# The third block of experts with up to 288 columns, computed in four quarters of the result's columns

## The chip, the cores and the metric

The kernel runs on one core of one Trainium2 chip. The metric is device time in microseconds (us) of one execution, as the median of several runs. The core's engines are named as in the profile: PE (TensorE, matmuls; PEld is its weight load), DVE (VectorE), ACT (ScalarE), POOL (GpSimd, which issues the indirect DMAs) and SP (SyncE, which issues the plain DMAs).

## What is computed

A macaron block over 8192 tokens (8 sequences of 1024) with 512 features, all in f32:

```python
x = x + 0.5 * ffn(layernorm(x))       # 32 experts, top-1, capacity 320
x = x + attention(layernorm(x))       # 16 heads of 32, rope, softmax
x = x + 0.5 * ffn(layernorm(x))       # the same experts again
```

The feed-forward part is where the change lies. Each token goes to the expert with the highest router probability, if it is among the first C = 320 tokens of that expert:

```python
C = ceil(1.25 * T / E)                                  # T = 8192, E = 32: 320
g = einsum("ech,ehf->ecf", buf, w_gate)
u = einsum("ech,ehf->ecf", buf, w_up)
y = einsum("ecf,efh->ech", silu(g) * u, w_down)
out_tok = where(accepted, y[slot] * gate, 0.0)
return xt + out_tok
```

All of H and F are 512. An expert's weights are three matrices of 512x512.

## The kernel before

The program has five parts in a row: a front that normalizes all tokens, computes the router's logits and writes a table of which token sits in which slot of which expert; a first expert stage; attention, which also routes the tokens for the second stage; a second expert stage; and nothing after it. The change touches only the expert stages.

**Widths.** The experts are sorted by their number of tokens, largest first (`sorted`). The number of columns of the expert of rank r is fixed when the program is built, in three lists (`Block.profiles`, lines 67 to 71); a value computed from the counts selects the first list that is wide enough (`arm`), and a switch (line 519) runs that one of three copies of the stage. With C = 320 and q = 32 the first list is ten experts of 320 columns, nine of 288, eight of 256 and five of 224; the second has only 320 and 256; the third only 320.

**Blocks.** An expert's tokens are taken in blocks of 128 partitions (`gather`, three indirect DMAs for over 256 columns, two else). A third block holds at most 64 tokens. So that its 128 partitions are used, the 64 tokens are there twice: `places` (line 554) reads the slot table as `rows`, copies the first 64 slots of each expert's third block over its last 64 (line 567), sorts it with a matmul against a permutation `matrix` (line 570), and writes three tables from the result: `come` (which token each partition gathers), `gates` (its gate), and `go` (which row of the output it writes). In the third block, partition half i writes row `2*token + i` of the output seen as rows of 256 (lines 574 to 579).

**One expert** (`feed`, line 712). PE's order is written out by hand, as is that of ACT, DVE and POOL (`manual_schedule`). For each of four slices f of the hidden columns: eight 128x128 weight tiles, four each for gate and up, as stationary operand, streamed against the transposed tokens `bT` (line 704, moving operand as wide as the expert), silu on ACT, and the product `a[:, f, :]` on DVE (line 728). Between f = 0 and f = 1 the next expert is normalized (`scales`, `normalize`), after f = 1 its `rests` are made. Then, block by block: six transposes of the next expert's tokens (line 692, before blocks 0 and 1), and the down product `yp`. In a full block `a` is the stationary operand, 128x128, and a slice of `wd` of 512 columns the moving one (line 745, four matmuls). In the third block (lines 751 to 757) `a`'s 64 columns are the stationary operand, once for each half of the result: half c of `wd`'s columns gives output partitions c*64 to c*64+63, 256 columns wide, so eight matmuls. DVE adds gate times `yp` to the residual (line 749; line 759 for the third block, with `rest`), and POOL scatters the 128 rows to the output (line 763).

**Rests** (line 669). The residual with its normalization is x scaled and shifted, per row. For full blocks it is made in place; for the third block, each half of the partitions takes its half of the columns into `rest` (two DVE instructions of 64x256).

**The start of a stage** (`experts`, lines 528 to 535). `places`, `gather` of expert 0, its weights, `begin` (statistics, normalization, twelve transposes at line 607, the copies to `bT` at line 611, and its rests), `gather` of expert 1, and then the loop over 32 experts with `feed`.

Of the kernel before, what the change touches and what calls it, by code (L numbers as in the profile page):

```python
# [13 lines left out]
F32 = mybir.dt.float32  # L14
# [3 lines left out]
ALU = mybir.AluOpType  # L18
# [4 lines left out]
P = 128  # L23
# [27 lines left out]
class Block:  # L51


    def __init__(self, nc, tc, T, D, E, F):
        self.nc, self.tc = nc, tc
        self.T, self.D, self.E, self.F = T, D, E, F
        self.NT, self.KD, self.KF = T // P, D // P, F // P
        self.C = int(math.ceil(CAPACITY_FACTOR * T / E))

        self.NB = -(-self.C // P)  # L60
        self.last = self.C - (self.NB - 1) * P
        assert E * self.NB <= P and self.last * 2 == P and D % 2 == 0
        self.NS = self.NB * E * P


        C, q = self.C, P // 4
        self.profiles = [
            [C] * 10 + [C - q] * 9 + [C - 2 * q] * 8 + [C - 3 * q] * (E - 27),
            [C] * 20 + [C - 2 * q] * (E - 20),
            [C] * E,  # L70
        ]
        assert all(widths[0] == widths[1] == C for widths in self.profiles)
        assert all(a <= b for one, two in zip(self.profiles, self.profiles[1:])
                   for a, b in zip(one, two))

        self.copy = nc.scalar.copy

# [424 lines left out]
    def experts(self, table, ranks, src, dst, weights, loaded=None, others=None):  # L502

        nc, tc, E = self.nc, self.tc, self.E
        views = dram_disjoint_views(dst, E * self.NB + (self.NT if others else 0))
        F = mybir.EngineType
        matrix, order, arm = ranks
        which = nc.values_load(
            arm[0:1, 0:1], min_val=0, max_val=len(self.profiles) - 1,
            skip_runtime_bounds_check_because="a sum of so many comparisons",
        )
        for i in tc.Switch(which, len(self.profiles)):
            widths = self.profiles[i]  # L520
            with (
                tc.tile_pool(name="ew", bufs=2) as wp,
                tc.tile_pool(name="ea", bufs=2) as ap,
                tc.tile_pool(name="eps", bufs=2, space=PSUM) as ps,
                tc.manual_schedule(engines={F.PE, F.Activation, F.DVE, F.Pool}),
            ):
                expert = Expert(self, (wp, ap, ps), src, views, others)
                expert.places(table, matrix)


                now = expert.gather(0, widths[0])
                now.weights = loaded or self.load(wp, order, 0, weights, hold="wu")
                expert.begin(now)
                following = expert.gather(1, widths[1])
                for r in range(E):
                    if following:
                        following.weights = self.load(
                            wp, order, r + 1, weights, hold=None if r else "wg"
                        )
                    after = None  # L540
                    if r + 2 < E:
                        after = lambda: expert.gather(r + 2, widths[r + 2])
                    now, following = following, expert.feed(now, following, after)


class Expert:
# [7 lines left out]
    def places(self, table, matrix):  # L554


        nc, s, ap, n = self.nc, self.s, self.ap, self.s.last
        E, R = s.E, s.NB * s.E
        self.come, self.go = (
            ap.tile([P, R], I32, tag=name, bufs=1, name=name) for name in ("come", "go")  # L560
        )
        ids, self.gates = (
            ap.tile([P, R], F32, tag=name, bufs=1, name=name) for name in ("ids", "gates")
        )
        rows = ap.tile([R, P, 2], F32, tag="slots", bufs=1, name="slots")
        nc.sync.dma_start(rows, table[0 : s.NS, :].rearrange("(r s) c -> r s c", s=P))
        nc.vector.tensor_copy(rows[R - E : R, n:P, :], rows[R - E : R, 0:n, :])
        for i, at in enumerate((ids, self.gates)):
            pt = self.ps.tile([P, R], F32, tag="tp", name="pt")
            nc.tensor.matmul(pt, rows[:, :, i], matrix, start=True, stop=True)  # L570
            if i == 0:
                nc.vector.tensor_scalar(self.come, pt, float(s.T - 1), None, ALU.min)
            nc.vector.tensor_copy(at, pt)
        nc.vector.tensor_copy(self.go[:, 0 : R - E], ids[:, 0 : R - E])
        for i in range(2):
            p = slice(i * n, (i + 1) * n)
            nc.vector.tensor_scalar(
                self.go[p, R - E : R], ids[p, R - E : R], 2.0, float(i), ALU.mult, ALU.add
            )

    def begin(self, to):

# [85 lines left out]

    def rests(self, to):

        s, n, half = self.s, self.s.last, self.s.D // 2
        for i in range(min(to.NB, s.NB - 1)):
            s.rest(to.x[:, i, :], to.x[:, i, :], to.by, i)
        if to.NB == s.NB:
            to.rest = self.ap.tile([P, half], F32, tag="rest", name="rest")
            for i in range(2):
                p = slice(i * n, (i + 1) * n)
                s.rest(
                    to.rest[p, :], to.x[p, s.NB - 1, i * half : (i + 1) * half], to.by,
                    s.NB - 1, p,  # L680
                )

# [29 lines left out]
    def feed(self, now, following, after):  # L712

        nc, s = self.nc, self.s
        n, half, KF = s.last, s.D // 2, s.KF
        a, wd = s.acts[now.r % 2], now.weights[2]
        others = self.fetch_others(now.r) if self.others else None
        if following:  # L720
            self.measure(following)
        later = after and after()
        for f in range(KF):
            sg, up = self.gated(now, f)
            if following and f == 0:
                self.scales(following)
                self.normalize(following)
            nc.vector.tensor_tensor(a[:, f, 0 : now.width], sg, up, ALU.mult)  # L728
            if following and f == 1:
                self.rests(following)  # L730
        if others:
            self.put_others(now.r, others)
        for i in range(now.NB):


            if following and i < 2:
                self.transpose(following, range(i * s.KD // 2, (i + 1) * s.KD // 2))
            yp = self.ps.tile([P, s.D], F32, tag="yp", name="yp")
            ys = self.ap.tile([P, s.D], F32, tag="ys", bufs=3, name="ys")
            gate = self.gates[:, i * s.E + now.r : i * s.E + now.r + 1]  # L740
            index = self.go[:, i * s.E + now.r : i * s.E + now.r + 1]
            to = self.views[now.r * s.NB + i]
            if i < s.NB - 1:
                for f in range(KF):
                    nc.tensor.matmul(  # L745
                        yp, a[:, f, i * P : (i + 1) * P], wd[:, f, :],
                        start=(f == 0), stop=(f == KF - 1),
                    )
                nc.vector.scalar_tensor_tensor(ys, yp, gate, now.x[:, i, :], ALU.mult, ALU.add)  # L749
            else:  # L750
                for f in range(KF):
                    for c in range(2):
                        nc.tensor.matmul(  # L753
                            yp[c * n : (c + 1) * n, 0:half], a[:, f, i * P : s.C],
                            wd[:, f, c * half : (c + 1) * half],
                            start=(f == 0), stop=(f == KF - 1),
                        )
                ys = ys[:, 0:half]
                nc.vector.scalar_tensor_tensor(
                    ys, yp[:, 0:half], gate, now.rest, ALU.mult, ALU.add  # L760
                )
                to = to.rearrange("t (c d) -> (t c) d", c=2)
            nc.gpsimd.indirect_dma_start(
                out=to, out_offset=bass.IndirectOffsetOnAxis(ap=index, axis=0),
                in_=ys, in_offset=None, bounds_check=to.shape[0] - 1, oob_is_err=False,
            )
        return later
# [730 lines left out]
```

## Time and profile before

| what | value |
|---|---|
| median of 3 runs | 4838.47 us (4837.74 to 4840.27) |
| the profiled execution | 4848.97 us |
| its span, first to last instruction | 4847.2 us |
| mean granted clock of PE | 0.974 |
| PE busy | 4596.5 us |
| DVE busy, ACT busy, POOL busy | 2836.3, 2923.5, 790.4 us |
| matmul records of line 753 (third block) | 608, busy 74.0 us together |
| matmul records of line 745 (full blocks) | 1024, busy 460.3 us together |
| DVE line 759 (third block's result) | 38, 483 ns each |
| DVE line 186, rest of 64x256 | 76, 412 ns each |

How to read the profile: times are counted from the span's start. The page divides the span into 40 slices and gives each engine's busy share of a slice in tenths. A line of the timeline has its start, its length, the engine, the line of the kernel, the operation, the tiles (out<-in), the shape and how many instructions were joined in it. An f32 matmul stands as two records of MATMUL and two of LDWEIGHTS. The shape `128*64 128x256` means 128 rows and 64 columns of stationary operand, and a moving operand of 256 columns. In brackets stands how long the engine was idle before, and what ended that. The chain is the work that ended last, followed back from the end: its shares say which engine and line set the time.

### The profile page before, as it was taken

How to read it: one execution, taken by the hardware profiler on the slowest of the kernel's cores; microseconds unless marked ns; L12 is line 12 of the kernel's file. 1: busy time of each engine (PE TensorE's matmuls, PEld its weight loads, DVE VectorE, ACT ScalarE, POOL GpSimd, SP SyncE). 2: the span in 40 equal slices, each digit the busy share in tenths (PEclk: the TensorE clock that was granted, in tenths of full speed). 3: DMA queues.
4: the chain of work that ended last, by engine and by line, in shares of the span. 5: the costliest groups of instructions: out<-in, count | busy, mean ns of one | idle time of the engine just before them, and what ended most of it. 6: DMA issues, size and time to landing. Idle time of an engine off the chain costs nothing.

```text
span 4847.2 us, 68820 instructions
## 1 busy us (share of the span) xinstructions
PE 4596.5 (95%) x24572; PEld 2128.0 (44%) x24572; DVE 2836.3 (59%) x5568; ACT 2923.5 (60%) x5856; POOL 790.4 (16%) x787
## 2 busy tenths in 40 slices
PE   6699999968999999999999999999999886999999
PEld 4466667722233333333333333333333234666677
DVE  8433333356666767767777767767767744333332
ACT  6221212128998888888888888888888841111111
POOL 4433333210000010110110110110110002222221
PEclk8799999979999999999999999999999997999999
DMA  4455566521111212212212212212212124455554
GB/s 142 148 187 184 190 197 220 178 85 29 34 30 60 75 38 65 70 42 65 70 42 65 70 42 65 69 42 66 60 43 57 49 70 154 158 174 177 171 193 137
DMA packets 290581, 486.02 MB, mean 100 GB/s; under 512 B 47895, under 2 KB 83169, under 8 KB 290224
## 3 DMA queue, kind: packets, MB, share of 16 engines
q1 hardware_dynamic: 255376, 404.36, 26.8%
q0 software_dynamic: 34560, 76.93, 5.2%
q8 instruction: 196, 3.21, 0.3%
q14 instruction: 161, 1.32, 0.1%
q10 hardware_dynamic: 288, 0.20, 0.0%
HBM read 380.11 MB, written 89.72 MB: 97 GB/s over the span
## 4 chain that ended last, share of the span: by engine, by line
PE 82%; DVE 7%; ACT 4%; issue 3%; DMA 2%; POOL 1%; SPq 1%; another core or an unknown queue 0%; DVEq 0%; POOLq 0%; ACTq 0%
PE sa L1220 13%; PE gp L704 10%; PE up L704 9%; PE pq L1125 9%; PE po L1302 9%; PE yp L745 9%; PE sb L1200 6%; PE px L1328 4%; PE pv L1170 4%; PE sb L1227 3%; ACT junk L1239 2%; DVE nm L1235 2%; PE tp L194 2%; DMA table<-row,slot 1%; PE yp L753 1%
## 5 line engine op out<-in xcount | busy, mean ns | idle before, releaser
L1235 DVE TENSOR_REDUCE nm<-sa 128x2 f32<-128x1024 f32 x1024 | 1248.7, 1220 | 648.3 <-PE sa L1220 386.9
L1239 ACT ACTIVATE junk<-sa,nm 128x512 f32<-128x512 f32 x2048 | 1407.3, 687 | 257.6 <-DVE nm L1235 177.0
L1220 PE MATMUL sa<-k,q 32*128 32x512 f32 x4096 | 1149.1, 645 | 17.9 <-ACT junk L1239 11.1
L1232 ACT ACTIVATE pr<-sb 128x1024 f32<-128x1024 f32 x1024 | 1040.5, 1018 | 101.3 <-PE sb L1227 97.4
L1227 PE MATMUL sb<-q,k 32*128 32x512 f32 x4096 | 1062.1, 602 | 0.0
L709 ACT ACTIVATE sg<-gp 128x320 f32<-128x320 f32 (+3 forms) x256 | 102.6, 401 | 1166.2 <-PE gp L704 1164.2
L1150 POOL TENSOR_TENSOR raw<-raw,a 128x512 f32<-128x512 f32 x128 | 164.2, 1283 | 2401.7 <-DMA rot<-raw 1645.0
L1302 PE MATMUL po<-pr,v 128*32 128x512 f32 x4096 | 548.0, 606 | 0.1
L704 PE MATMUL gp<-bT,wg 128*128 128x320 f32 (+3 forms) x2048 | 530.7, 402 | 0.0
L704 PE MATMUL up<-bT,wu 128*128 128x320 f32 (+3 forms) x2048 | 524.8, 399 | 0.0
L1125 PE MATMUL pq<-hT,wqk 128*128 128x512 f32 x1024 | 511.3, 624 | 4.9 <-DVE raw L1140 3.9
L745 PE MATMUL yp<-wd,a 128*128 128x512 f32 x1024 | 460.3, 592 | 0.0
L704 PEld LDWEIGHTS gp<-bT,wg 128*128 128x128 f32 x2048 | 386.7, 190 | 115.7 <-issue 26.7
L1200 PE MATMUL sb<-mrow,ones 3*128 3x512 bf16 x2048 | 392.9, 384 | 42.0 <-ACT pr L1232 40.7
L728 DVE TENSOR_TENSOR a<-sg,up 128x320 f32<-128x320 f32 (+3 forms) x256 | 114.0, 445 | 541.6 <-PE up L704 371.1
L704 PEld LDWEIGHTS up<-bT,wu 128*128 128x128 f32 x2048 | 388.9, 190 | 94.1
L1200 PEld LDWEIGHTS <-ones 3*128 3x128 bf16 x2048 | 99.6, 91 | 709.6 <-issue 670.1
L1239 ACT ACTIVATION_READ_ACCUMULATOR junk<-sa,nm 128x1 f32 x2048 | 398.2, 194 | 0.0
L1227 PEld LDWEIGHTS sb<-q,k 32*128 32x128 f32 x4096 | 359.7, 184 | 0.1
L1220 PEld LDWEIGHTS sa<-k,q 32*128 32x128 f32 x4096 | 304.9, 184 | 81.3 <-ACT pr L1232 30.3
L1125 PEld LDWEIGHTS pq<-hT,wqk 128*128 128x128 f32 x1024 | 176.2, 191 | 323.8 <-issue 227.0
L749 DVE SCALAR_TENSOR_TENSOR ys<-yp,gates,x 128x512 f32<-128x512 f32 x128 | 96.1, 751 | 336.8 <-PE yp L745 336.8
(178 smaller groups left out, 4241.8 us busy)
## 6 DMA issues: line engine op xcount, KB each, us to landing
wg<-in_w_gate SPq DMA_DIRECT2D x64, 1024.0 KB
wu<-in_w_up SPq DMA_DIRECT2D x64, 1024.0 KB
wd<-in_w_down SPq DMA_DIRECT2D x64, 1024.0 KB
rot<-raw SPq DMA_DIRECT2D x1024, 32.0 KB
all<-in_x SPq DMA_DIRECT2D x32, 512.0 KB
xt<-first_rows SPq DMA_DIRECT2D x64, 256.0 KB
xr<-first_rows SPq DMA_DIRECT2D x64, 256.0 KB
d<-inverse SPq DMA_DIRECT2D x256, 64.0 KB
```

The costliest lines, as they stand in the source:

```text
L704: nc.tensor.matmul(acc, w[:, k, f * P : (f + 1) * P], to.bT[:, k, 0:width], start=(k == 0), stop=(k == s.KD - 1),)
L745: nc.tensor.matmul(yp, a[:, f, i * P : (i + 1) * P], wd[:, f, :], start=(f == 0), stop=(f == KF - 1),)
L1125: nc.tensor.matmul(acc, w[:, which, k, :], self.hT[b, n][:, k, :], start=(k == 0), stop=(k == KD - 1),)
L1170: nc.tensor.matmul(acc, hT[:, k, at : at + P], self.w_vo[:, k, :], start=(k == 0), stop=(k == KD - 1),)
L1200: nc.tensor.matmul(sb[:, h, :], self.ones16[at : at + 3, :], row[at : at + 3, :], start=True, stop=False,)
L1220: nc.tensor.matmul(sa[:, h, :], qa[at, (g * 4 + j) * P : (g * 4 + j + 1) * P], ka[at, m * 512 : (m + 1) * 512], start=True, stop=True,)
L1227: nc.tensor.matmul(sb[:, h, :], k[at, t * P : (t + 1) * P], q[at, n * 512 : (n + 1) * 512], start=False, stop=True,)
L1232: nc.scalar.activation(pr, sb, AF.Exp)
L1235: nc.vector.tensor_reduce(nm[:, m, j, pair : pair + 2], sa, AX.X, ALU.max, negate=True)
L1239: nc.scalar.activation(self.junk, sa[:, h - pair, :], AF.Exp, bias=nm[:, m, j, h : h + 1], accum_out=se[:, m, j, h : h + 1],)
L1302: nc.tensor.matmul(self.po[at : at + HD, :], self.v[b][t][:, c * P + at : c * P + at + HD], prs[h // 2 * 2][:, h % 2, :], start=(t == 0), ...
L1328: nc.tensor.matmul(acc, self.oT[b, c, half][:, j * P : (j + 1) * P], self.w_vo[:, c, :], start=False, stop=(c == KD - 1),)
```

## The change

A third block with at most 32 tokens (an expert of at most 288 columns, `quarter`) has its tokens there four times, once for each quarter of the result's columns. `parts(width)` is 1, 4 or 2: 1 up to 256 columns, 4 up to 288, else 2. In the first list of widths the nine experts of 288 columns are concerned; in the other lists none.

- `places` is as before; a new step, `quarters`, follows after the gather of expert 1. It repeats the first 32 slots of the third blocks four times, sorts them with two small matmuls for the ranks concerned only, and writes these ranks' columns of `come`, `go` (`4*token + k` for partition quarter k) and `gates` again.
- `rests` makes four pieces of 32x128 instead of two of 64x256 for these experts.
- In `feed` the third block's product is, for these experts, sixteen matmuls with a stationary operand of 128x32 and a moving operand of 128 columns, each into 32 output partitions; the result is 128x128, and its rows are scattered into the output seen as rows of 128.

```diff
+        self.quarter = (self.NB - 1) * P + P // 4
...
                 following = expert.gather(1, widths[1])
+                expert.quarters(widths)
...
+    def parts(self, width):
+        s = self.s
+        return 1 if width <= (s.NB - 1) * P else 4 if width <= s.quarter else 2
+
+    def quarters(self, widths):
...
+        few = [r for r, width in enumerate(widths) if self.parts(width) == 4]
+        if not few:
+            return
...
+        rows = ap.tile([R, 4, n * 2], F32, tag="four", bufs=1, name="four")
+        nc.vector.tensor_copy(
+            rows[last, :, :],
+            self.rows[last, 0:n, :].rearrange("r s c -> r (s c)").unsqueeze(1)
+            .to_broadcast([E, 4, n * 2]),
+        )
+        rows = rows.rearrange("r k (s c) -> r (k s) c", c=2)
+        for i in range(2):
+            pt = self.ps.tile([P, len(few)], F32, tag="tp", name="pt")
+            nc.tensor.matmul(
+                pt, rows[last, :, i], self.matrix[last, at], start=True, stop=True
+            )
+            if i == 0:
+                nc.vector.tensor_scalar(self.come[:, at], pt, float(s.T - 1), None, ALU.min)
+                for k in range(4):
+                    p = slice(k * n, (k + 1) * n)
+                    nc.vector.tensor_scalar(
+                        self.go[p, at], pt[p, :], 4.0, float(k), ALU.mult, ALU.add
+                    )
+            else:
+                nc.vector.tensor_copy(self.gates[:, at], pt)
...
     def rests(self, to):
...
-            for i in range(2):
+        if parts > 1:
+            n, d = P // parts, s.D // parts
+            to.rest = self.ap.tile([P, s.D // 2], F32, tag="rest", name="rest")
+            for i in range(parts):
                 p = slice(i * n, (i + 1) * n)
                 s.rest(
-                    to.rest[p, :], to.x[p, s.NB - 1, i * half : (i + 1) * half], to.by,
+                    to.rest[p, 0:d], to.x[p, s.NB - 1, i * d : (i + 1) * d], to.by,
                     s.NB - 1, p,
                 )
...
                 for f in range(KF):
-                    for c in range(2):
+                    for c in range(parts):
                         nc.tensor.matmul(
-                            yp[c * n : (c + 1) * n, 0:half], a[:, f, i * P : s.C],
-                            wd[:, f, c * half : (c + 1) * half],
+                            yp[c * n : (c + 1) * n, 0:part], a[:, f, i * P : i * P + n],
+                            wd[:, f, c * part : (c + 1) * part],
                             start=(f == 0), stop=(f == KF - 1),
                         )
...
-                to = to.rearrange("t (c d) -> (t c) d", c=2)
+                to = to.rearrange("t (c d) -> (t c) d", c=parts)
```

More of the change, by code (lines that the diff above doesn't have):

```diff
@@ L564, in places @@
         )
-        rows = ap.tile([R, P, 2], F32, tag="slots", bufs=1, name="slots")
+        self.matrix = matrix
+        self.rows = rows = ap.tile([R, P, 2], F32, tag="slots", bufs=1, name="slots")
         nc.sync.dma_start(rows, table[0 : s.NS, :].rearrange("(r s) c -> r s c", s=P))
@@ L579, in places @@
             )
+    def parts(self, width):
+        s = self.s
+        return 1 if width <= (s.NB - 1) * P else 4 if width <= s.quarter else 2
+    def quarters(self, widths):
+        nc, s, ap = self.nc, self.s, self.ap
+        E, R, n = s.E, s.NB * s.E, P // 4
+        few = [r for r, width in enumerate(widths) if self.parts(width) == 4]
+        if not few:
+            return
+        assert few == list(range(few[0], few[-1] + 1)) and few[0] > 1
+        last = slice(R - E, R)
+        at = slice(R - E + few[0], R - E + few[-1] + 1)
+        rows = ap.tile([R, 4, n * 2], F32, tag="four", bufs=1, name="four")
[19 more added lines that the diff above has]
+                nc.vector.tensor_copy(self.gates[:, at], pt)
     def begin(self, to):
@@ L669, in rests @@
     def rests(self, to):
-        s, n, half = self.s, self.s.last, self.s.D // 2
+        s, parts = self.s, self.parts(to.width)
         for i in range(min(to.NB, s.NB - 1)):
             s.rest(to.x[:, i, :], to.x[:, i, :], to.by, i)
-        if to.NB == s.NB:
-            to.rest = self.ap.tile([P, half], F32, tag="rest", name="rest")
-            for i in range(2):
+        if parts > 1:
+            n, d = P // parts, s.D // parts
+            to.rest = self.ap.tile([P, s.D // 2], F32, tag="rest", name="rest")
+            for i in range(parts):
                 p = slice(i * n, (i + 1) * n)
                 s.rest(
-                    to.rest[p, :], to.x[p, s.NB - 1, i * half : (i + 1) * half], to.by,
+                    to.rest[p, 0:d], to.x[p, s.NB - 1, i * d : (i + 1) * d], to.by,
                     s.NB - 1, p,
@@ L716, in feed @@
         nc, s = self.nc, self.s
-        n, half, KF = s.last, s.D // 2, s.KF
+        KF, parts = s.KF, self.parts(now.width)
+        n, part = P // parts, s.D // parts
         a, wd = s.acts[now.r % 2], now.weights[2]
@@ L751, in feed @@
                 for f in range(KF):
-                    for c in range(2):
+                    for c in range(parts):
                         nc.tensor.matmul(
-                            yp[c * n : (c + 1) * n, 0:half], a[:, f, i * P : s.C],
-                            wd[:, f, c * half : (c + 1) * half],
+                            yp[c * n : (c + 1) * n, 0:part], a[:, f, i * P : i * P + n],
+                            wd[:, f, c * part : (c + 1) * part],
                             start=(f == 0), stop=(f == KF - 1),
                         )
-                ys = ys[:, 0:half]
+                ys = ys[:, 0:part]
                 nc.vector.scalar_tensor_tensor(
-                    ys, yp[:, 0:half], gate, now.rest, ALU.mult, ALU.add
+                    ys, yp[:, 0:part], gate, now.rest[:, 0:part], ALU.mult, ALU.add
                 )
-                to = to.rearrange("t (c d) -> (t c) d", c=2)
+                to = to.rearrange("t (c d) -> (t c) d", c=parts)
             nc.gpsimd.indirect_dma_start(
```

## The prediction, made before the changed kernel was run

> **What bounds the kernel now.** I read the page first, then the chain of work that ended last inside the expert stages, then the timeline around one third block, then the timeline and the granted clock where an expert stage starts. The page:
>
> ```profile
> span 4847.2 us, 68820 instructions
> PE 4596.5 (95%) x24572; PEld 2128.0 (44%) x24572; DVE 2836.3 (59%) x5568; ACT 2923.5 (60%) x5856; POOL 790.4 (16%) x787
> PE   6699999968999999999999999999999886999999
> ```
>
> The expert stages fill slices 3 to 8 and the last six; PE stands at 9 in all of them. A 95% share is an average, so I asked for the chain from 200 to 696 us, which is nearly all experts with a third block of the first stage:
>
> ```profile
> by line: PE gp L704 31.2%; PE up L704 30.4%; PE yp L745 26.3%; PE yp L753 7.2%; PE tp L692 4.9%
> ```
>
> These five are 100% and all PE: no transfer and no other engine ends a wait there. The second stage (4062 to 4566 us) reads the same within 0.5 points. So in these stages a nanosecond off PE is a nanosecond off the time, and what PE waits for is lost whole. The block that is changed, and what follows it, for the last 320-column expert:
>
> ```profile
> 459.88 0.59 PE L745 MATMUL yp<-wd,a 128*128 128x512 f32 x1
> 460.40 1.49 PEld L753 LDWEIGHTS yp<-wd,a 128*64 128x64 f32 x16 [0.76 <-issue]
> 460.40 1.95 PE L753 MATMUL yp<-wd,a 128*64 128x256 f32 x16
> 462.27 1.75 PEld L704 LDWEIGHTS gp<-bT,wg 128*128 128x128 f32 x8 [0.38 <-issue]
> ```
>
> From its first weight load to the next expert's is 1.87 to 1.88 us; in all 38 experts with three blocks it is the same.
>
> **The third block, per expert.** An f32 matmul is two records. Today: 8 matmuls, 16 records, two tiles of 64 columns side by side, so 8 rounds; rounds 2 and 8 start at 460.67 and 461.96, so a round of 256 columns takes 1.29 / 6 = 0.216 us. 8 x 0.216 = 1.73, and 0.15 is left for filling, the second tile's offset and a pause of 0.09 before the next full-width load. After: 16 matmuls, 32 records, again 8 rounds if four tiles of 32 columns run side by side, each of 128 columns. The length of a round follows the columns: L745 starts every 0.430 us at 512, L753 every 0.216 at 256, the transposes of L692 every 0.108 at 128. That four tiles run side by side is seen in the attention stage:
>
> ```profile
> L1302 PEld LDWEIGHTS po<-pr,v x4096: 106/109/153, 1127.9 to 3961.9; 128*32 128x32 f32 x196
> L1302 PE MATMUL po<-pr,v x4096: 592/617/1062, 1127.9 to 3962.3; 128*32 128x512 f32 x196
> ```
>
> There the eight records from 2004.69 on take 1.07 us together while one takes 0.6: four start within 0.03 us, the other four 0.43 us later. So the block becomes 8 x 0.109 = 0.87, plus 0.02 for four offsets, 0.03 for the first load and the same 0.09: 1.01 us. Saved: 1.87 - 1.01 = 0.86 us.
>
> How many: the L704 gp records of 128x288 are 576, at 32 for an expert: 18 experts, 9 in each stage, which are the ones concerned (both stages took the first of the three lists of widths). 18 x 0.86 = 15.5 us off.
>
> [...] The trace shows starts 5 to 7 ns apart within a round, but only in short bursts: the densest 64 consecutive PE instructions that I count (LDWEIGHTS and MATMUL, in attention) take 2.86 us, and the new block wants 64 in about 1. [...]
>
> **Beside PE, per expert.** Rests: two of 64x256 (0.41 each) become four of 32x128. Between 0.17 (go, 64x32) and 0.41, by columns, about 0.28 each: 1.11 for 0.83 us. DVE is idle for 1.74 us behind them (472.55 to 474.29, waiting for PE's up), which hides 0.28; even four at 0.41 would fit. Without that cover it would be 5 us in all. The product's eviction (L759) halves its columns: 0.48 to about 0.35 (L749: 0.75 at 512). The scatter keeps 128 rows, half as long; POOL's issue of 0.98 us is per instruction. Gathers and weight loads are not touched. None of these is on the chain: nothing.
>
> **The new step at the start of each stage.** It is placed after begin() of expert 0, so in PE's order two small matmuls stand ahead of the first gp, and wait for a DVE copy ("four") that stands behind the rests. Before:
>
> ```profile
> 185.85 0.92 DVE L611 COPY bT<-tp 128x320 f32<-128x320 f32 x2 [1.34 <-PE tp L607]
> 186.39 3.47 PE L704 MATMUL gp<-bT,wg 128*128 128x320 f32 x8
> 186.68 1.13 DVE L186 TENSOR_SCALAR x<-x,r,n 128x512 f32<-128x512 f32 x2
> 187.73 0.82 DVE L186 TENSOR_SCALAR rest<-x,r,n 64x256 f32<-64x256 f32 x2
> 188.59 0.69 DVE L151 BATCH_NORM_STATS2 st<-x 128x6 f32<-128x512 f32 x1
> ```
>
> gp starts when bT is there, and the four rests run beside it. After: the copy starts at 188.6, takes about 0.26 (L567, half as long: 0.22), PE starts 0.1 later at 188.95; its four loads come every 0.213 us as at L570 (four in 0.93), so gp follows at 189.8. That is 3.4 us later; 0.2 comes back, since gp no longer waits for ACT's share of bT. In the second stage the rests end at 4060.25 and gp, now at 4057.87, would start at 4061.5: 3.6, less 0.2. Queued behind PE's wait is all of the stage. On DVE, the six writes that follow (0.17 to 0.26 each) push the statistics of expert 1 by 2.2 us, less than PE's own shift; POOL and SP keep their order.
>
> The pause also costs clock:
>
> ```profile
> core 0: us, PE busy (x) PEld busy (x) DVE busy (x) ACT busy (x) POOL busy (x), PEclk, DMA share, GB/s
> 186.39:188.55 2.16, 2.16 (x5) 1.51 (x5) 2.15 (x5) 1.80 (x3) 1.45 (x2) 0.50 0.56 142
> 188.55:191.96 3.41, 3.41 (x14) 2.38 (x13) 2.11 (x6) 0.44 (x1) 0.54 (x2) 1.00 0.74 237
> 4055.85:4059.26 3.41, 3.30 (x11) 2.53 (x12) 2.08 (x7) 2.51 (x5) 2.29 (x3) 0.50 0.86 312
> 4059.26:4062.68 3.42, 3.42 (x14) 2.40 (x13) 2.62 (x7) 0.87 (x2) 1.03 (x2) 1.00 0.80 213
> ```
>
> In this trace the granted clock changes only at multiples of 3.41 us, and here it rose at the end of a stretch of that length that PE had filled (3.30 of 3.41 in the second stage). Today the transposes and gp make that stretch together, and gp spends 2.16 and 1.39 us at half clock. With the hole, the stretch has to come from gp alone: 2.2 to 5.5 us at half clock, so 0 to 2 us more. I take 0.9, the middle. A stage's start then costs 3.2 to 5.4, taken as 4.2: 8.4 for both.
>
> **Sum.** -15.5 + 8.4 = -7.1 us. On the profiled execution 4848.97 (span 4847.2 and 1.8 around it) becomes 4841.9; its distance of 10.5 to the median of the runs shown, 4838.47, should stay, so 4831.4.
>
> **Rivals.** What a measurement of this kernel can tell from no change is about 0.2%, 9.7 us.
> A, the hole is cheap: the clock rises after one window and a start costs 2.7: -15.5 + 5.4 = -10.1, 4828.4. For it: the window from 188.55 would be 88% busy. Against: a quarter of it are 9-column matmuls. 0.16.
> B, rounds longer than their columns: the four loads are issued only behind four matmuls, 0.027 + 0.109 = 0.136 a round, block 1.23, saved 0.64 x 18 = 11.5: -3.1, 4835.4. 0.12.
> C, slower: PE cannot be fed 64 instructions in a microsecond. The gain is gone at a block of 1.41 us (1.88 less 8.4 / 18), about 40 ns for a matmul; beyond 0.2% it is slower from 1.95 us. [...] Against: the bursts. 0.20, of which a third stays below 4850.
> D, the change doesn't do what it says: the loads are not hidden, or the tiles take turns in pairs; block 1.88, only the starts are left: +8.4, 4846.9. 0.08.
> The sum above: 0.44, own range 4828.9 to 4834.
>
> **Chances.** Faster is A, 0.16; the same is the sum, B and D, 0.64; slower is C, 0.20. The range from 4827 to 4850 leaves out most of C and a little of A.
>
> **What will show it.** The new yp line: 576 matmul records of 128x128, mean spacing 27 ns, and 1.0 us from its first load to the next gp (1.23 is B, 1.9 D, above 1.95 C). The period of a 288-column expert: 24.9 us instead of 25.78. At the starts: two pt matmuls waiting for DVE's "four", gp 3.2 to 3.6 us later behind the transposes, and the time at which the clock goes to 1.00. Wrong would be a wait of DVE's a (L728) on the rests, or PE idle in front of gp for a transfer, in the narrow experts.

## The result and the profile after

| | median us | runs | lowest to highest |
|---|---|---|---|
| before | 4839.88 | 20 | 4837.38 to 4844.36 |
| after | 4830.89 | 20 | 4827.32 to 4837.47 |

The ratio is 0.9982, with a 95% interval from 0.9976 to 0.9989: 5 to 12 us less, about 9. The forecast was 4831.4 us, and 7.1 us less.

The page of the changed kernel, whose profiled execution took 4828.91 us:

```profile
span 4827.0 us, 69461 instructions
PE 4583.2 (95%) x24868; PEld 2125.8 (44%) x24868; DVE 2844.0 (59%) x5618; ACT 2925.9 (61%) x5856; POOL 790.8 (16%) x787
PE   6699999878999999999999999999999886999999
```

PE has 13 us less to do and DVE 8 us more; ACT and POOL are within 3 us of what they were. The chain in the same stretch of the first stage (193 to 681 us, the experts of rank 0 to 18):

```profile
by line: PE gp L746 31.8%; PE up L746 30.8%; PE yp L788 26.8%; PE yp L796 5.7%; PE tp L734 5.0%
```

It is still all PE, and the third block (L753 before, now L796) went from 7.2% to 5.7%. (All lines behind the new functions stand 41 to 43 further down: L704 is L746, L745 is L788, L607 is L648.) One block of a 288-column expert in the timeline, and what follows it:

```profile
478.43 0.59 PE L788 MATMUL yp<-wd,a 128*128 128x512 f32 x1
478.95 0.81 PEld L796 LDWEIGHTS yp<-wd,a 128*32 128x32 f32 x32 [0.76 <-issue]
478.96 1.08 PE L796 MATMUL yp<-wd,a 128*32 128x128 f32 x32
479.97 1.02 PEld L746 LDWEIGHTS gp<-bT,wg 128*128 128x128 f32 x5 [0.20 <-issue]
480.11 0.35 DVE L802 SCALAR_TENSOR_TENSOR ys<-yp,gates,rest 128x128 f32<-128x128 f32 x1 [0.29 <-PE yp L796]
```

From the block's first weight load to the next expert's it is 478.95 to 479.97; in single records 1.010 to 1.011 us, in all 18 blocks. The 20 blocks still in halves take 1.877 us as before. An expert of 288 columns takes 24.91 us from its first matmul to the next expert's, where it took 25.78. The price is paid where a stage starts; the first stage:

```profile
174.66 0.92 DVE L652 COPY bT<-tp 128x320 f32<-128x320 f32 x2 [1.33 <-PE tp L648]
...
176.57 0.84 DVE L189 TENSOR_SCALAR rest<-x,r,n 64x256 f32<-64x256 f32 x2
...
177.33 0.28 DVE L601 COPY four<-slots 32x256 f32<-32x256 f32 x1
177.72 0.92 PEld L609 LDWEIGHTS pt<-matrix,four 32*128 32x128 f32 x4 [2.85 <-issue]
...
178.66 0.50 PEld L746 LDWEIGHTS gp<-bT,wg 128*128 128x128 f32 x2
178.67 3.71 PE L746 MATMUL gp<-bT,wg 128*128 128x320 f32 x7
```

DVE's first copy to bT ends at about 175.1. In the kernel before, gp began at this point; here it begins at 178.66. The two small matmuls stand ahead of it (L609, 177.72), and they wait for "four" (177.33), which stands on DVE behind the rests (176.57). From the last transpose to "four" PE has nothing to do; this wait is called the hole from here on. The granted clock, as the trace recorded it behind the two starts:

```profile
178.66:181.85 3.19, 3.19 (x7) 2.18 (x7) 2.96 (x10) 0.00 (x0) 0.00 (x0) 0.50 0.90 303
181.85:184.00 2.15, 2.15 (x9) 1.50 (x8) 0.58 (x5) 1.13 (x2) 1.07 (x2) 1.00 1.04 399
4043.35:4049.15 5.80, 5.80 (x12) 3.83 (x12) 3.54 (x14) 1.12 (x3) 1.86 (x2) 0.50 1.01 370
4042.33:4045.74 3.41, 3.31 (x9) 2.52 (x10) 2.48 (x11) 0.00 (x0) 0.00 (x0) 0.50 0.88 267
```

The first and third lines reach from gp's first load to the clock's rise. PE is busy in all of both, with 7 matmul records in 3.19 us at clock 0.50 and, after the rise, 9 in 2.15 us at 1.00. The last line is the stretch of 3.41 us that ends one such length before the rise at 4049.15: PE filled 3.31 us of it, and the clock did not rise at its end.

The account of the two traces, stage by stage, follows. "gp" is the time from the start of begin()'s last transpose to gp's first load, "half" the time at clock 0.50 from there on, "stage" the time from gp's first load to the start of the last expert's last matmul. Each entry is first stage / second stage.

| | gp, us | half, us | stage, us |
|---|---|---|---|
| before | 0.36 / 0.36 | 2.16 / 1.39 | 777.96 / 777.58 |
| after | 3.82 / 4.00 | 3.18 / 5.80 | 770.67 / 771.96 |

Blocks: 9 x 0.867 = 7.80 less in each stage, 15.6 in all. Waits: 3.46 and 3.64 more. Half clock: half of 1.02 and of 4.41, so 0.51 and 2.21 more. The stages agree with it: 777.96 - 7.80 + 0.51 = 770.67, and 777.58 - 7.80 + 2.21 = 771.99. In all -15.6 + 9.8 = -5.8 us, which lies in the measured interval of 5 to 12.

The spans of the two profiles differ by 20.2 us, and most of that is not the change: 11.2 us lie in the front, ahead of all that was touched (see the end), and 3.1 us between the two stages, a stretch that takes between 3088.8 and 3097.5 us in the eleven traces shown here. What is left are the 5.8 us of the account.

### The profile page after: what moved, and what is told of

It reads as the page before. It is cut to its first block, busy times and chain, and to the rows that moved or that the text cites. A ratio compares the mean times of both kernels' runs of the same rounds, so it can differ in the third digit from the quotient of the medians.

```text
span 4827.0 us, 69461 instructions
## 1 busy us (share of the span) xinstructions
PE 4583.2 (95%) x24868; PEld 2125.8 (44%) x24868; DVE 2844.0 (59%) x5618; ACT 2925.9 (61%) x5856; POOL 790.8 (16%) x787
## 3 DMA queue, kind: packets, MB, share of 16 engines
q14 instruction: 160, 1.31, 0.1%
## 4 chain that ended last, share of the span: by engine, by line
PE 83%; DVE 7%; ACT 4%; issue 2%; DMA 2%; POOL 1%; SPq 1%; DVEq 0%; POOLq 0%; ACTq 0%
PE sa L1263 14%; PE gp L746 10%; PE up L746 10%; PE po L1345 9%; PE pq L1168 9%; PE yp L788 9%; PE sb L1243 6%; PE px L1371 4%; PE pv L1213 4%; PE sb L1270 3%; ACT junk L1282 2%; DVE nm L1278 2%; PE tp L197 2%; PE tp L734 1%; DMA table<-row,slot 1%
## 5 line engine op out<-in xcount | busy, mean ns | idle before, releaser
L746 PE MATMUL gp<-bT,wg 128*128 128x320 f32 (+3 forms) x2048 | 532.7, 403 | 0.0
L746 PE MATMUL up<-bT,wu 128*128 128x320 f32 (+3 forms) x2048 | 525.5, 399 | 0.0
L788 PE MATMUL yp<-wd,a 128*128 128x512 f32 x1024 | 460.3, 592 | 0.0
L746 PEld LDWEIGHTS gp<-bT,wg 128*128 128x128 f32 x2048 | 387.6, 191 | 112.4 <-issue 24.9
L771 DVE TENSOR_TENSOR a<-sg,up 128x320 f32<-128x320 f32 (+3 forms) x256 | 114.2, 446 | 540.3 <-PE up L746 507.3
L746 PEld LDWEIGHTS up<-bT,wu 128*128 128x128 f32 x2048 | 389.5, 190 | 94.6 <-issue 0.8
```

The source lines that it names most:

```text
L746: nc.tensor.matmul(acc, w[:, k, f * P : (f + 1) * P], to.bT[:, k, 0:width], start=(k == 0), stop=(k == s.KD - 1),)
L788: nc.tensor.matmul(yp, a[:, f, i * P : (i + 1) * P], wd[:, f, :], start=(f == 0), stop=(f == KF - 1),)
```

## The experiments

The experiments were run in three groups on different chips. The kernel before was run beside each group, so a ratio compares one chip with itself, and times of different groups are not to be compared. Before took 4839.16 us (44 runs) beside e1_early, e2_step_alone, e6_copy_early and e4_twice; 4848.61 us (9 runs) beside e9_half_columns, e7_rests_twice and e5_filled; and 4851.3 us (9 runs) beside e8_warm and e1_again.

| kernel | median us | ratio to before, 95% interval | gp, us | half, us | stage, us |
|---|---|---|---|---|---|
| e1_early | 4822.85 | 0.9965 (0.9951 to 0.9978) | 0.36 / 0.36 | 3.20 / 3.74 | 770.67 / 770.94 |
| e2_step_alone | 4846.35 | 1.0015 (1.0008 to 1.0021) | 3.82 / 4.00 | 5.92 / 5.47 | 779.82 / 779.60 |
| e6_copy_early | 4826.33 | 0.9974 (0.9963 to 0.9984) | 1.31 / 1.31 | 4.47 / 3.00 | 771.31 / 770.57 |
| e4_twice | 4847.17 | 1.0017 (1.0010 to 1.0024) | 3.82 / 4.00 | 4.47 / 3.99 | 779.16 / 778.93 |
| e9_half_columns | 4821.20 | 0.9942 (0.9928 to 0.9956) | 0.36 / 0.36 | 1.25 / 2.66 | 765.87 / 766.57 |
| e7_rests_twice | 4831.56 | 0.9962 (0.9949 to 0.9976) | 0.36 / 0.36 | 2.49 / 3.84 | 770.32 / 771.00 |
| e5_filled | 4839.82 (one run) | | 3.43 / 3.62 | 0 / 0 | 769.11 / 769.11 |
| e8_warm | 4830.15 | 0.9953 (0.9940 to 0.9967) | 0.53 / 0.36 | 0 / 1.27 | 769.11 / 769.72 |
| e1_again | 4834.16 | 0.9961 (0.9948 to 0.9975) | 0.36 / 0.37 | 0.99 / 3.69 | 769.58 / 770.92 |

The theory is the sum of the prediction: what 18 shorter blocks save of PE's time, less what PE's wait and its half clock cost at two starts.

**The blocks without the price of the start** (e1_early):

```diff
                 now = expert.gather(0, widths[0])
+                expert.quarters(widths)
...
                 following = expert.gather(1, widths[1])
-                expert.quarters(widths)
```

> The new step is put between the gather of expert 0 and its begin(), where PE and DVE wait for the gathered tokens. Theory (PE's sum: 18 blocks shorter by 0.867 us, and two starts that cost 3.5 us of waiting and 0.5 to 2.2 us of half clock each): the starts cost nothing, the blocks still 1.01 us, so the kernel before less 15.6 us, a ratio of 0.9968; gp follows the last transpose by 0.4 us as before. Rival (the step costs by its own instructions, wherever it stands, or the early writes delay the gather): as the changed kernel, 0.998, or slower. Rival (the measured gain came from a shorter front, not from the blocks): 0.998 as well.

Measured: 0.9965, 17 us less than before (11 to 24). The step now stands where PE and DVE wait for the gathered tokens, and gp follows bT at once, 0.36 us behind the last transpose, as in the kernel before:

```profile
164.60 0.28 DVE L601 COPY four<-slots 32x256 f32<-32x256 f32 x1
164.93 0.92 PEld L609 LDWEIGHTS pt<-matrix,four 32*128 32x128 f32 x4 [1.28 <-DVE four L601]
...
168.11 0.69 DVE L154 BATCH_NORM_STATS2 st<-x 128x6 f32<-128x512 f32 x1 [1.53 <-DMA x<-in_x,come]
...
174.51 0.92 DVE L652 COPY bT<-tp 128x320 f32<-128x320 f32 x2 [1.34 <-PE tp L648]
...
175.06 0.50 PEld L746 LDWEIGHTS gp<-bT,wg 128*128 128x128 f32 x2 [0.34 <-DVE bT L652]
```

DVE still waits 1.53 us for the gathered tokens after all of the step's writes: it costs nothing there. Of the rivals, a price of the instructions as such is out. So is a gain from a shorter front: the two stages themselves, which don't contain the front, are 7.29 and 6.64 us shorter than before. The version is faster than before and, it seems, than the changed kernel: their two intervals just touch (up to 0.9978 here, from 0.9976 there), and e1_again, the same kernel on another chip, has 0.9961 (0.9948 to 0.9975).

**The price of the start without the blocks** (e2_step_alone): the kernel before, with `quarters` behind `gather(1)` as in the change, writing to tables of its own.

```diff
                 following = expert.gather(1, widths[1])
+                expert.quarters(widths)
...
+        come, go = (
+            ap.tile([P, R], I32, tag=name, bufs=1, name=name) for name in ("come2", "go2")
+        )
```

> The kernel before with the new step alone, in its place behind begin(), writing into tables that nothing reads; the third blocks stay in halves. Theory: gp starts 3.4 to 3.7 us later in each stage and spends 0 to 2 us more at half clock, nothing of it comes back: 7 to 11 us slower, a ratio of 1.0015 to 1.0023. Rival (PE has slack later in the stage that takes the hole in): 1.0000.

Measured: 1.0015, 7 us slower (4 to 10), at the lower edge of what was expected. gp starts 3.46 and 3.64 us later, exactly as in the changed kernel, and nothing of it comes back in the stages. Its own trace adds up to more, 7.1 us of waiting and 3.9 of half clock, 11.0 together, just outside what was measured; the half clock differs from execution to execution (see "The half clock"). Together e1_early (-17) and e2_step_alone (+7) give -10, against -9 measured for the change.

**Which part of the step** (e6_copy_early): only the copy "four", taken out of `quarters`, goes ahead of begin().

```diff
                 now = expert.gather(0, widths[0])
+                expert.repeat(widths)
...
```

> The changed kernel with only the DVE copy 'four' put before begin(); the two small matmuls and the writes stay behind it. Theory: PE does not wait any more, only the two matmuls stand ahead of gp: four loads at half clock, 0.85 us, less the 0.2 us that gp then does not wait for ACT; the work has no hole and the clock rises as before. So 0.7 us a start where the changed kernel pays 4 to 6: before less 14, a ratio of 0.9971. Rival (what costs is not the wait for the copy but the wait for a free PSUM tile or the writes behind it): as the changed kernel, 0.998.

Measured: 0.9974 (0.9963 to 0.9984). The time does not decide, since the rival's 0.998 lies in the interval too. The trace does: the two small matmuls follow the transposes without a hole, and gp follows them.

```profile
175.13 1.02 PE L617 MATMUL pt<-matrix,four 32*128 32x9 f32 x4
176.08 1.44 PE L754 MATMUL gp<-bT,wg 128*128 128x320 f32 x2
```

gp is 0.95 us later than before at each start, where the changed kernel has 3.46 and 3.64. So 2.5 to 2.7 us of each start are the wait for the copy behind the rests, and 0.95 the two matmuls (expected 0.85). The rival, a wait that stays with the matmuls, is out. Two expectations failed: the 0.2 us back from ACT did not come, and the clock did not rise as in the kernel before, but after 4.47 and 3.00 us of gp instead of 2.16 and 1.39.

**Is PE fed?** (e4_twice):

```diff
-                for f in range(KF):
+                for f in list(range(KF)) * (2 if parts == 4 else 1):
                     for c in range(parts):
```

> The changed kernel with the sixteen matmuls of each quartered third block made twice in a row, the second pass over the first, so 128 PE instructions in one run. Theory (rounds of 0.109 us, PE is fed fast enough): eight rounds more for each block, 0.87 us x 18 = 15.7 us more than the changed kernel, a ratio to before of 1.0014. Rival (the short block lives on a queue filled beforehand; at the pace of the densest 64 instructions of attention, 45 ns each, the second 64 take 2.9 us): 30 to 50 us more than the changed kernel, a ratio of 1.005 to 1.009.

Measured: 1.0017, where the changed kernel has 0.9982: 17 us more (12 to 22), or about 0.9 us for each block. 15.7 were expected, 30 or more by the rival. In the trace the doubled block takes 1.88 us, 0.87 more, and the second half is as fast as the first:

```profile
479.29 1.96 PE L796 MATMUL yp<-wd,a 128*32 128x128 f32 x64
481.17 2.21 PE L746 MATMUL gp<-bT,wg 128*128 128x288 f32 x8
```

That is 128 records (64 of matmuls and 64 of their loads) in 1.88 us, 15 ns for each. PE is fed at this pace for twice as long as the change asks.

**What sets a round** (e9_half_columns; half of each quarter's columns of the result are left out):

```diff
+                some = part // 2 if parts == 4 else part
...
-                            yp[c * n : (c + 1) * n, 0:part], a[:, f, i * P : i * P + n],
-                            wd[:, f, c * part : (c + 1) * part],
+                            yp[c * n : (c + 1) * n, 0:some], a[:, f, i * P : i * P + n],
+                            wd[:, f, c * part : c * part + some],
...
```

> The version with the step put early, and in it each of the sixteen matmuls of a quartered block streams 64 columns instead of 128, so half of these blocks' result is left out (its place takes the rests alone). Theory as the prediction had it (the length of a round follows the streamed columns): rounds of 0.056 us, a block of 0.59 us, 18 x 0.43 = 7.7 us less than the version with the step put early, 0.9949. Rival (four weight loads of 32 columns take about as long as the 128 columns stream, and bound the round below that): rounds stay at 0.107 to 0.112, the block at 1.0 us, 0.9965. Rival (PE's feeding bounds 64 instructions): also about 1.0 us.

Measured: 0.9942 (0.9928 to 0.9956) where 0.9949 was expected, against 0.9962 for e7_rests_twice on the same chip, whose blocks are whole. These intervals overlap (0.9949 is the other's lower end), so the trace has to tell. The block:

```profile
485.60 0.49 PEld L797 LDWEIGHTS yp<-wd,a 128*32 128x32 f32 x32 [0.76 <-issue]
485.60 0.65 PE L797 MATMUL yp<-wd,a 128*32 128x64 f32 x32
486.19 0.78 PEld L746 LDWEIGHTS gp<-bT,wg 128*128 128x128 f32 x4
```

It takes 0.58 us, with rounds of 0.056 where 128 columns take 0.109, as the columns alone say. A weight load's record still lasts 109 ns here, nearly two rounds. So neither the four weight loads nor the feeding sets the rounds of 0.109 us in the change; even 64 records in 0.58 us are taken.

**Is the work beside PE hidden?** (e7_rests_twice):

```diff
-            for i in range(parts):
+            for i in list(range(parts)) * (2 if parts == 4 else 1):
                 p = slice(i * n, (i + 1) * n)
                 s.rest(
```

> The version with the step put early, and in it the four rests of each quartered expert made twice over (eight DVE instructions of 32x128 instead of four, 1.3 us more for each of 18 experts). Theory (nothing beside PE is on the path; DVE stands idle for 1.15 us behind the rests and its next product has a second PSUM tile as slack): as the version with the step put early, 0.9965. Rival (DVE's extra work holds up PE): up to 18 x 1.3 = 24 us more, a ratio up to 1.0015.

Measured: 0.9962 (0.9949 to 0.9976), as e1_early and e1_again; the rival's 1.0015 is out. In the timeline of DVE the eight rests reach up to the next product:

```profile
496.47 1.00 DVE L189 TENSOR_SCALAR x<-x,r,n 128x512 f32<-128x512 f32 x2
497.38 2.93 DVE L189 TENSOR_SCALAR rest<-x,r,n 32x128 f32<-32x128 f32 x8
500.34 0.45 DVE L771 TENSOR_TENSOR a<-sg,up 128x288 f32<-128x288 f32 x1
```

L771, the product, no longer waits for PE but comes at once behind the rests, and the stages still take 770.32 and 771.00 us. The four rests of the change have more room than they use.

**The half clock** (e5_filled): three matmuls of 224 columns in the hole of the changed kernel.

```diff
...
+        fill = self.ps.tile([P, s.D], F32, tag="yp", name="fill")
+        for j in range(3):
+            nc.tensor.matmul(
+                fill[:, 0:224], now.b[:, 0, 0:P], now.b[:, 0, 224:448], start=True, stop=True
+            )
```

> The changed kernel with three matmuls of 224 columns, whose result nothing reads, put between the transposes and the two small matmuls of each stage's start, where PE waits for the DVE copy. Theory: gp starts as late as in the changed kernel (3.8 to 4.0 us behind the last transpose), but PE has no hole, so the clock rises 1.4 to 3.7 us after the start of gp as in the kernel before, where the changed kernel shows 3.2 and 5.8. In time 1 us a start at most, less than one look can tell. Rival (the clock's rise doesn't depend on the hole): 3 to 6 us after gp, as in the changed kernel.

Measured: the clock was up 2.3 and 2.4 us before gp, earlier than expected, and both stages took 769.11 us. The first start, as the stretch from the clock's rise to gp (clock 1.00) and two lines of its timeline:

```profile
187.49:189.79 2.30, 1.37 (x9) 1.03 (x7) 1.71 (x7) 1.05 (x1) 1.47 (x3) 1.00 0.64 191
189.26 0.61 PE L614 MATMUL pt<-matrix,four 32*128 32x9 f32 x4 [0.93 <-DVE four L601]
189.80 2.42 PE L751 MATMUL gp<-bT,wg 128*128 128x320 f32 x8
```

769.11 us is the stage at full clock. Every stage of the table with quartered blocks made once and in whole is 769.1 plus half of its time at half clock, to within 0.05 us (for the changed kernel's first stage 769.11 + 3.18 / 2 = 770.70, and 770.67 was measured). The rival, a rise that doesn't depend on what PE does before gp, is out. The time itself, one run, tells nothing.

How much half clock the step behind begin() adds is seen only over many starts. The six starts in the traces that have it (this kernel as changed, e2_step_alone, e4_twice) spent 3.18 to 5.92 us of gp at half clock, 4.8 on average. The ten in which gp follows the last transpose by 0.36 us (before, e1_early, e9_half_columns, e7_rests_twice, e1_again) spent 0.99 to 3.84, 2.5 on average. Half of the difference is 1.1 us a start, and with it the account reads -15.6 + 7.1 + 2.3 = -6.2 us for the change and +9.4 for e2_step_alone, both within what was measured.

Whether the hole alone does this is not shown. The two starts of e6_copy_early have the small matmuls and no hole, and lie between, at 4.47 and 3.00 us. In the stretch 4042.33 to 4045.74 of the changed kernel, shown with the result, PE's records fill 3.31 of 3.41 us without a rise, but four of the nine are the matmuls of 9 columns. So the narrow matmuls are a rival to the hole for a part of the price, and no run here has the hole without them.

**Filling in front** (e8_warm, and e1_again beside it): the early step, and then four matmuls of 480 columns in the wait for the first tokens.

```diff
...
+        fill = self.ps.tile([P, s.D], F32, tag="yp", name="fill")
+        for j in range(4):
+            nc.tensor.matmul(
+                fill[:, 0:480], s.before,
+                s.rev.rearrange("p g e -> p (g e)").unsqueeze(1).to_broadcast([P, 2, G * E])[:, :, 0:240],
+                start=True, stop=True,
+            )
```

> The version with the step put early, and behind the step four matmuls of 480 columns whose result nothing reads, in the 6 us in which PE waits for the first gathered tokens. Theory (what is left of a start's price is half clock): the clock is up when the transposes come, so the last eight of them take 0.9 us less, and gp loses nothing where the version with the step put early loses half of 3.2 and 3.7 us: 2.5 us a stage, 5 us in all, a ratio of 0.9955 where that version has 0.9965, and stages of 769.1 us. Rival (PE's clock falls again in the pause before the transposes, or the filling delays them): no gain, 0.9965 or more.

> The version with the step put early once more, beside the one with the filling on the same chip: 0.9965 again, stages of 770 to 771 us.

Measured: 0.9953 against 0.9961, with intervals that overlap, so the times don't tell the two apart. In the trace theory and rival each have one stage: in the first the clock was up 2.9 us before gp and the stage took 769.11 us; in the second it rose at 4043.0, fell at 4046.4, and rose again 1.27 us after gp began. The second stage, as two stretches (clock 1.00, then 0.50) and a line of its timeline:

```profile
4042.96:4046.37 3.41, 1.61 (x7) 0.60 (x5) 1.54 (x10) 1.45 (x2) 1.09 (x2) 1.00 1.00 376
4046.37:4049.78 3.41, 3.18 (x11) 2.41 (x12) 2.08 (x7) 2.51 (x5) 2.18 (x3) 0.50 0.82 295
4046.60 1.97 PE L655 MATMUL tp<-ident,b 128*128 128x128 f32 x8 [1.89 <-ACT b L175]
```

Between rise and fall PE ended the filling (4043.9), made four transposes (to 4044.7) and then waited 1.89 us for ACT.

## Why the prediction was right

- **The block**, 1.01 us and 0.86 us saved: 1.011 and 0.867. What it was added up from held too: four tiles side by side (starts 6 to 7 ns apart), rounds of 0.109 us at 128 columns, the same 0.09 us before the full-width load. e9_half_columns and e4_twice show two terms on their own: rounds of 0.056 us at 64 columns, and 128 records at 15 ns each.
- **How many**: 18, and each the same.
- **Beside PE: nothing.** Right, though a rest of 32x128 takes 0.34 us, not 0.28: four take 1.45 us, and DVE then waits for PE for 1.15 us in most of the experts, 0.79 at the least. The scatter and the product's eviction (0.35 us, as estimated) show nowhere on the chain.
- **The wait at the start**, 3.4 and 3.6 us: 3.46 and 3.64. The term beside it failed: "0.2 comes back, since gp no longer waits for ACT's share of bT". Nothing came back. The profile puts 0.20 us of idle time before gp's third load down to ACT's bT, but the same 0.20 us stands before the loads after it, and before the third load of the changed kernel, where bT has long been there. From gp's first load to its third it is 0.70 us in both kernels (186.39 to 187.09 before, 178.66 to 179.36 after).
- **The half clock**, 0.9 us for a start: 0.51 and 2.21 in the two traces compared, so 2.7 for both starts instead of 1.8, and 1.1 a start as the mean over all traces. The 5.80 us in the second stage lie above the forecast's range of 2.2 to 5.5 us: the forecast took a stretch of 3.41 us that PE fills to be enough for a rise, which was the author's estimate from two starts; at the end of the one from 4042.33 on (3.31 of 3.41 us) none came. With work of PE ahead of gp in e5_filled the rise came 2.3 and 2.4 us before gp, where in the changed kernel it came 3.18 and 5.80 us after gp's start; which part of the price is the hole's and which the narrow matmuls' stays open.
- **The sum** in the trace is -5.8 for a forecast of -7.1: 0.5 us more of waiting and 0.9 more of half clock, less 0.1 for the blocks. The time came out at -9.0, and both lie within the measured interval.
- **How close it came is in part luck.** 4830.89 is within 0.6 us of 4831.4, but the forecast was put on a median of 4838.47 us from three runs, and the twenty runs of before gave 4839.88. The base was 1.4 us too low and the gain 1.9 us too small, and these nearly cancel.
- **The profile against the median.** "Its distance of 10.5 to the median of the runs shown should stay" failed: the changed kernel's profile lies 2.0 us below its median. The forecast of the time was not touched by it, since the sum was put on the median.
- **The rivals.** The time alone does not separate the sum (-7.1) from A (-10.1), since 5 to 12 us less allows both; the traces do. A (a start for 2.7 us) did not happen: 4.0 and 5.9 there, and 4.7 with the mean half clock. B, C and D all change the block, and it is 1.01. C's premise, that no stretch of the old trace was dense enough, was true and said nothing about the limit: e4_twice took 128 records at 15 ns each. The third of C's chance that was put below 4850 us rests on a pace of feeding that no run shows. Neither of the two signs of being wrong showed: in all 18 experts the product waited for PE and not for the rests, and PE waited for no transfer in either stage.

## What to carry to other kernels

Matmuls with small stationary operands, placed side by side in column tiles, cost here what their moving columns cost: 0.109 us for a round of four at 128 columns and 0.056 at 64, also for 128 records in a row. What a column costs could be read off the wider matmuls of the old trace (0.430 us at 512 columns, 0.216 at 256). What a change adds once, at a stage's start, has to be followed through each engine's order: here a step whose 0.28 us copy stood behind other DVE work took back about half of the gain, and the same instructions about 13 us earlier, in a wait that was there anyway, cost nothing (gp 0.36 us behind the last transpose, as before). Such a step in front of PE's work cost here its length (3.5 us) and, on top, about 1.1 us for the longer time at half clock.

## What the runs showed of the hardware that was not expected

- The front, which no kernel here changes, is 11 us longer on some chips: the first matmul of `places` starts at 173.97 us in the profile of before and at 163.00 in that of after, and the kernel before takes 4839 us on one chip and 4849 to 4851 on two others. DVE's instructions of the two traces are about 0.5 us apart or less up to 117 us and fall apart in several steps from there (4 us at 129, 7 at 145, 11 at 156). Why is open.
- Matmuls of 64 columns in four tiles kept a pace of 0.056 us a round with all weight loads hidden, though a load's record lasts 109 ns (e9_half_columns).
- The granted clock fell over a wait of PE of only 1.89 us: in the second stage of e8_warm it was up for only 3.41 us, and PE was busy for 1.61 of them.
- Some stretches of 3.41 us that PE's records fill were not followed by a rise: besides the one shown with the result, three in a row in the attention stage of the kernel before (1103.3 to 1113.6 us, matmuls on 32 rows) are full, with the clock at 0.50 in all and in the 3.41 us behind them. What the rise follows is open.
